# A graph attention layer on one core: weighted rows in a tile of their own, a carry that reads the sum ahead of its copy, and nine products without readers

## The chip, the core and the metric

The kernel runs on one core of a Trainium2 chip. A core has five engines with queues of their own: TensorE (PE in the profile, with PEld for its weight loads), VectorE (DVE), ScalarE (ACT), GpSimd (POOL) and SyncE (SP). They work in the order of their own queues and wait for each other by semaphores. The metric is the device time of one execution in microseconds; less is better.

## What is computed

One layer of graph attention over 12,500 nodes with 128 features and 200,000 edges that are sorted by destination.

```python
h = jnp.maximum(_layernorm(x), 0.0)
h = (h @ W_node.T).reshape(num_nodes, H, HD)              # H, HD = 4, 32
e = (edge_features @ W_edge.T).reshape(num_edges, H, HD)
att = jnp.sum(jnp.concatenate([h[src], h[tgt], e], -1) * a, axis=-1)
att = jnp.where(att > 0, att, 0.2 * att)
m = jnp.maximum(segment_max(att, tgt), 0.0)
ex = jnp.exp(att - m[tgt])
denom = segment_sum(ex, tgt) + (num_edges - deg)[:, None] * jnp.exp(-m)
h_prime = segment_sum((ex / denom[tgt])[:, :, None] * h[src], tgt)
out = x + h_prime.reshape(num_nodes, H * HD)
```

The sums divide by the denominator of the destination, so the kernel sums `ex * h[src]` and `ex` by destination and divides at the end.

## The kernel before, in words

**Tiling.** The sorted edges are cut into 392 groups of 511, each laid out as 512 places in four columns of 128 partitions (J = 4); the first place of a group holds what is carried in from the group before. A group's destinations fall into a window of at most 96 nodes (WIN). Four groups are a quad (98 quads), and two to four quads are a turned stage (`supers`: mostly four quads, 16 groups).

**First part.** Node features are normalised, multiplied by the weights and written to a table in DRAM, 137 numbers a row: the values with a one behind each head, a count, and the source's part of the logits (`R_SRC`). The first four quads gather raw rows of `x` meanwhile and convert them on the chip (`converted`).

**Gathers.** `gather` (L128) issues 16 indirect transfers per quad on POOL's queue (L137), one for each column of each group, into `ga`. This tile has room for eight quads (QUADS), that is 32 groups; the transfer into a group's slot must wait for the last use of that slot 32 groups earlier. `fetch(q + 2)` is called when the logits of quad q are opened.

**Logits.** `logits` (L493), for one group: DVE marks the destination of each edge (L500), TensorE picks the destination's part by these marks (L505) and adds the edge's part (L508). `add_sources` (L511), called by `flush` when the next quad's logits begin, reduces them and adds the source's part (L520, L522).

**Softmax, one turned stage at a time** (`softmax`, L533). The logits of up to 16 groups and four heads are turned so that edges lie along a row (L548); ACT makes 0.2 times the logits and DVE takes the larger (L550, L553); scans along the rows give the running maxima (L557, L582, L584), with two tiny products that move a column to a row and back (L564, L577); the exponentials are turned back (L600), as are the factors and the maxima of segment ends (L605, L610).

**Sums** (`sums`, L668), a step for each group: DVE weights the gathered rows in place, `ga` times `ex` (L687), and makes a one-hot matrix of the edges' windows places (L691). TensorE multiplies columns 1 to 3 of the group (L696, three products). Then `complete` (L621) finishes the group before it: DVE takes the last row of the sum before that one, scales it and writes it as the first row of `ga` (L634), ACT adds the count (L638), TensorE multiplies column 0 with it (L639), and ACT copies the finished sum from PSUM to SBUF (L640). This carry links each group to the next. After four groups `divide` (L701) makes the quotient on DVE and SP writes it out (L724).

**Order.** The order is written by hand: `together` runs the steps of several generators in turns. In a turned stage, the sums of one quad run beside the logits of a quad four or five ahead, and in the first quad of the stage also beside the softmax. So DVE's queue is, per group, L500, L687, L691, L634; PE's is L505 and L508, L696, L639; ACT's is L640 and L638. SP's queue holds, per quad, the loads of edges and destinations (L283, L285), four register loads (L458), eight window transfers (L468, L470), and four times a register load and a write of the result (L724).

Of the kernel before, what the change touches and what calls it, by code (L numbers as in the profile page):

```python
# [26 lines left out]
J = 4  # L27
# [19 lines left out]
def kernel(  # L47
# [68 lines left out]
    thru = consts.tile([1, G], F32, name="thru")  # L116
    flag = consts.tile([1, 1], I32, name="flag")
# [30 lines left out]
    with tc.manual_schedule():  # L148
# [88 lines left out]
        def converted(q, psum, turn_pool, copy):  # L237

            ga = GA[q]
            m = quads[q][1]  # L240
            made = []

            def turned_over(i):
                hT_ps = psum.tile([P, 512], F32, name="acc")
                hT_ps = hT_ps.rearrange("p (j e) -> p j e", j=J)
                for j in range(J):
                    nc.tensor.transpose(hT_ps[:, j, :], ga[:, i, j, 0:D], ident)
                hT = turn_pool.tile([P, J, P], F32, name="hT_e", bufs=2)
                copy(hT, hT_ps)
                made.append(hT)  # L250

            turned_over(0)
            for i in range(m):
                yield
                if i + 1 < m:
                    turned_over(i + 1)
                for k in range(J // 2):
                    row_ps = psum.tile([P, 512], F32, name="acc")
                    row_ps = row_ps.rearrange("p (j e) -> p j e", j=2)
                    for j in range(2):  # L260
                        nc.tensor.matmul(row_ps[:, j, :ROW], made[i][:, 2 * k + j, :],
                                         wcat, start=True, stop=True)
                    nc.scalar.copy(ga[:, i, 2 * k:2 * k + 2, :], row_ps[:, :, :ROW])
            rows = ga[:, :m].rearrange("p g j r -> p (g j) r")
            nc.scalar.copy(
                rows[:, :, 0:H * HW].rearrange("p t (h w) -> p t h w", w=HW)[:, :, :, HD],
                ones[:, 0:1].unsqueeze(2).to_broadcast([P, m * J, H]))
            nc.scalar.copy(rows[:, :, R_CNT], ones[:, 0:m * J])
            yield
# [18 lines left out]
        with tc.tile_pool(name="node", bufs=2) as node, tc.tile_pool(  # L288
# [10 lines left out]
            def indexed():  # L299
# [27 lines left out]
                yield  # L327

# [109 lines left out]
    with tc.tile_pool(name="work", bufs=2) as work, \  # L438
# [7 lines left out]
        share_ps = const_ps[0:WIN, WIN + G:].rearrange("p (g h) -> p g h", h=H)  # L446
        nc.vector.tensor_copy(lane_ps, lane)
        nc.vector.tensor_copy(node_ps, node_at)
        tops = consts.tile([1, H, len(supers) + 1], F32, name="tops")
# [7 lines left out]
        def window(g):  # L457
            return nc.values_load(  # L458
                base[0:1, g:g + 1], engines=[mybir.EngineType.SP], min_val=0, max_val=N - 1,
                skip_runtime_bounds_check_because="a destination, which is a node")  # L460

        def fetch_windows(q):
            g0, m = quads[q]
            pw = PW[q] = load.tile([WIN, QG, SIDE], BF16, name="pw")
            xw = XW[q] = work.tile([WIN, QG, D], F32, name="xw", bufs=8)
            at = [window(g0 + i) for i in range(m)]
            for i in range(m):
                nc.sync.dma_start(pw[:, i, :], side[bass.ds(at[i], WIN), :])  # L468
            for i in range(m):
                nc.sync.dma_start(xw[:, i, :], x[bass.ds(at[i], WIN), :])  # L470
# [14 lines left out]
        def open_logits(q):  # L485
            if q == supers[of_quad[q]][0]:
                fetch_rows(of_quad[q])
            if q + 2 < nq:
                fetch(q + 2)
            AT[q] = work.tile([WIN, QG, GE], BF16, name="at")  # L490
            LG[q] = ps.tile([P, QG, J, PIECES, H], F32, name="lg")
# [40 lines left out]

        def softmax(s):  # L533
# [11 lines left out]
            u = U.pop(s)  # L545
            t_ps = ps.tile([SBG * H, GE], F32, name="t_ps")
# [3 lines left out]
            nc.scalar.mul(low[:R], t_ps[:R, 1:GE], SLOPE)  # L550
            yield
            att = t_ps[:R, 1:GE]
            nc.vector.tensor_tensor(att, att, low[:R], op=OP.max)  # L553
# [23 lines left out]
            nc.tensor.matmul(col_ps, into[:, :R], ones[0:1, 0:1], start=True, stop=True)  # L577
            yield
# [7 lines left out]
            ex = turned.tile([SBG * H, GE], F32, name="ex")  # L586
# [20 lines left out]
            nc.scalar.copy(facs[:, :R], fac_ps)  # L607
# [3 lines left out]
            xs = turned.tile([P, J, SBG * H], F32, name="xs", bufs=2)  # L611
            nc.scalar.copy(xs[:, :, 0:R], top_ps)
# [5 lines left out]
        begun = []  # L618
        state = {}

        def complete():  # L621

            division = state.pop("division", None)
            if begun:
                complete_group(*begun.pop())
            if division:
                divide(*division)

        def complete_group(q, i, ga, hot, pt, acc, fc):
            g0, m = quads[q]  # L630
            g = g0 + i
            if g:
                before = state["before"]
                nc.vector.tensor_tensor(  # L634
                    ga[0:1, i, 0, 0:H * HW].rearrange("p (h w) -> p h w", w=HW),
                    before[WIN:WIN + 1, 0:H * HW].rearrange("p (h w) -> p h w", w=HW),
                    fc.unsqueeze(2).to_broadcast([1, H, HW]), op=OP.mult)
                nc.scalar.copy(ga[0:1, i, 0, R_CNT:R_CNT + 1], before[WIN:WIN + 1, R_CNT:R_CNT + 1])  # L638
            nc.tensor.matmul(acc, hot[:, i, 0, :], ga[:, i, 0, :], start=False, stop=True)  # L639
            nc.scalar.copy(pt[:, i, :], acc)  # L640
            state["before"] = acc

            part = 1 if q == nq - 1 else 2 if q == nq - 2 else QG
            if (i + 1) % part == 0 or i == m - 1:
# [4 lines left out]
                state["division"] = q, pt, den, lo, i + 1  # L649
# [6 lines left out]
        def marks(q):  # L656

            g0, m = quads[q]
            hot = work.tile([P, QG, J, WIN + 1], F32, name="hot", bufs=3)
# [8 lines left out]
        def sums(q):  # L668
# [10 lines left out]
            for i in range(m):  # L679
                nc.scalar.copy(ga[:, i, :, R_SRC:R_SRC + H], heads(xs)[:, :, :, g0 - s0 + i])  # L680
            for i in range(m):
                g = g0 + i
                if q == nq - 1 - FREE and i == 1:
                    for k in range(FREE):
                        HOT[nq - FREE + k] = marks(nq - FREE + k)
                val = ga[:, i, :, 0:H * HW].rearrange("p j (h w) -> p j h w", w=HW)
                nc.vector.tensor_tensor(  # L687
                    val, val, heads(ex)[:, :, :, g - s0].unsqueeze(3).to_broadcast([P, J, H, HW]),
# [6 lines left out]
                for j in range(1, J):  # L695
                    nc.tensor.matmul(acc, hot[:, i, j, :], ga[:, i, j, :], start=j == 1, stop=False)  # L696
                complete()
                begun.append((q, i, ga, hot, pt, acc, fc[:, :, g - s0]))
                yield

        def divide(q, pt, den, lo, hi):  # L701
# [20 lines left out]
            add.tensor_tensor(res[:, :n, :], res[:, :n, :], xw, op=OP.add)  # L722
            for i in range(n):
                nc.sync.dma_start(out[bass.ds(window(quads[q][0] + lo + i), WIN), :], res[:, i, :])  # L724

        def all_logits(q):
            flush()
            open_logits(q)
            for i in range(QG):
# [16 lines left out]
        def checked():  # L746
# [17 lines left out]
            for k, (g0, n) in enumerate(blocks(G, P)):  # L764
                rows = turned.tile([P, NE + 1], I32, name="rows")
                nc.scalar.dma_start(rows[:n], dst_rows[g0:g0 + n, 0:NE + 1])
                yield
# [16 lines left out]
        with tc.manual_schedule():  # L784
# [8 lines left out]
            for s, (q0, m) in enumerate(supers):  # L793
# [17 lines left out]
                if not s:  # L811
                    complete()
                    together(*late(3))
            flush()
            together(sums(nq - 1))
            complete()
            complete()
# [199 lines left out]
```

## Time and profile before

| what | value |
|---|---|
| three runs | 2570.87, 2578.58, 2586.93 us |
| profiled execution | 2600.19 us |
| its span, first to last instruction | 2598.4 us |
| busy: PE, PEld, DVE, ACT, POOL | 1405.4, 1256.7, 1367.0, 421.7, 1508.0 us |
| mean granted clock of TensorE | 0.536 |
| POOL's gathers from the table (L137) | 1502, 944 ns each (median), 161.1 to 2472.0 us |
| DMA | 299.12 MB, mean 115 GB/s |

Lines of the profile name an engine, a line of the kernel, the operation, and what is written and read (`acc<-ga,hot`), with the number of instructions and the time. In a list of waits a line says which engine idled before which instruction, whose signal ended that, and then the total in us, the number of waits and the longest. "remote" stands where the profile does not name the one that gave the signal, "issue" where it shows no wait. The end of a product of TensorE is modelled in these records; when its signal came is seen at the instruction that waits for it.

### The profile page before, as it was taken

To read this page: it belongs to the slowest core of one execution; us is meant where nothing else is said; L and a number is where in the kernel's file an instruction comes from. 1 tells how busy PE (TensorE), PEld (TensorE's weight loads), DVE (VectorE), ACT (ScalarE), POOL (GpSimd) and SP (SyncE) were. 2 spreads that over 40 slices of the span, in tenths; PEclk is the share of its full clock that TensorE was granted. 3 is DMA by queue.
4 is the path that set the end of the run, shared out by engine and by line. 5 is a ranking of instruction groups with operands and counts; after the bars stand their busy time and mean duration, and the time that the engine had idled before them with its cause. 6 is when DMAs were issued, how large, how long until landed. Compare 5 with 4: busy or idle time off the path is not lost. (4 is left out here: it accounts for less than half of the span.)

```text
span 2598.4 us, 29393 instructions
## 1 busy us (share of the span) xinstructions
PE 1405.4 (54%) x7275; PEld 1256.7 (48%) x7275; DVE 1367.0 (53%) x3291; ACT 421.7 (16%) x1806; POOL 1508.0 (58%) x1609
## 2 busy tenths in 40 slices
PE   2442665555555555556555555655555555545485
PEld 1331655545545445445445544545544554444375
DVE  2441465555555545555554554654554554555486
ACT  1431411111111111111111111111111111111122
POOL 7235256666666666666666666666666666666603
PEclk9975655555555555555555555555555555555555
DMA  4342455544544454554455445454544544434430
GB/s 150 102 126 53 108 136 124 127 116 118 128 123 113 115 142 107 127 125 117 119 124 124 116 119 123 120 125 117 125 115 118 125 121 116 121 97 112 103 92 17
DMA packets 214495, 299.12 MB, mean 115 GB/s; under 512 B 86121, under 2 KB 162153, under 8 KB 204914
## 3 DMA queue, kind: packets, MB, share of 16 engines
q1 hardware_dynamic: 162512, 184.97, 26.6%
q0 software_dynamic: 50112, 109.65, 19.3%
q10 hardware_dynamic: 1698, 2.58, 0.3%
q8 instruction: 61, 1.00, 0.2%
q14 instruction: 112, 0.92, 0.1%
HBM read 270.49 MB, written 26.52 MB: 114 GB/s over the span
## 5 line engine op out<-in xcount | busy, mean ns | idle before, releaser
L137 POOL DMA_INDIRECT ga<-table,srci x1502 | 1426.7, 950 | 963.2 <-issue 406.0
L696 PE MATMUL acc<-ga,hot 128*97 128x137 f32 x2352 | 649.6, 448 | 341.3 <-ACT ga L680 225.1
L696 PEld LDWEIGHTS acc<-ga,hot 128*97 128x97 f32 x2352 | 518.2, 279 | 366.1 <-ACT ga L680 229.2
L634 DVE TENSOR_TENSOR ga<-acc,facs 1x132 f32<-1x132 f32 x391 | 115.9, 296 | 625.9 <-ACT pt L640 502.1
L639 PE MATMUL acc<-ga,hot 128*97 128x137 f32 x784 | 267.4, 444 | 289.0 <-ACT ga L638 215.5
L508 PE MATMUL lg<-wblk,ea 128*128 128x8 f32 x1568 | 410.5, 360 | 0.0
L508 PEld LDWEIGHTS lg<-wblk,ea 128*128 128x128 f32 x1568 | 383.3, 310 | 0.0
L505 PEld LDWEIGHTS <-at 96*128 96x128 bf16 x1568 | 219.7, 167 | 298.7 <-DVE at L500 115.0
L639 PEld LDWEIGHTS acc<-ga,hot 128*97 128x97 f32 x784 | 190.3, 279 | 320.3 <-ACT ga L638 235.8
L640 ACT COPY pt<-acc 97x137 f32<-97x137 f32 x392 | 107.4, 274 | 1431.8 <-remote 850.5
L505 PE MATMUL lg<-pw,at 96*128 96x12 bf16 x1568 | 170.7, 182 | 239.1 <-DVE at L500 101.2
L687 DVE TENSOR_TENSOR ga<-ga,ex_ps 128x528 f32<-128x528 f32 x392 | 270.0, 689 | 8.4 <-remote 8.0
L500 DVE TENSOR_TENSOR at<-const_ps,db 96x512 bf16<-96x512 f32 x392 | 267.1, 683 | 9.0 <-DMA db<-in_dst_dram 3.2
L691 DVE TENSOR_TENSOR hot<-const_ps,slot 128x384 f32<-128x384 f32 x384 | 209.4, 545 | 0.0
L520 DVE TENSOR_REDUCE st<-lg 128x64 f32<-128x192 f32 x98 | 35.0, 358 | 139.1 <-remote 109.7
L638 ACT COPY ga<-acc 1x1 f32<-1x1 f32 x391 | 59.9, 153 | 228.8 <-DVE ga L634 114.1
L375 PE MATMUL row_ps<-wcat,hT 128*128 128x137 f32 x198 | 40.3, 354 | 79.9 <-DVE hT L367 32.0
L600 PE MATMUL ex_ps<-ident,ex 64*128 64x64 f32 (+2 forms) x112 | 18.6, 315 | 115.6 <-ACT ex L589 49.7
L375 PEld LDWEIGHTS row_ps<-wcat,hT 128*128 128x128 f32 x198 | 34.0, 246 | 86.1 <-issue 46.0
L553 DVE TENSOR_TENSOR t_ps<-t_ps,low 64x511 f32<-64x511 f32 (+2 forms) x28 | 19.2, 687 | 104.4 <-issue 60.2
L137 POOL DMA_INDIRECT ga<-in_x_dram,srci x64 | 60.6, 947 | 20.9 <-issue 19.2
L600 PEld LDWEIGHTS ex_ps<-ident,ex 64*128 64x128 f32 (+2 forms) x112 | 13.8, 208 | 118.3 <-ACT ex L589 51.1
(131 smaller groups left out, 1131.1 us busy)
## 6 DMA issues: line engine op xcount, KB each, us to landing
db<-in_dst_dram SPq DMA_DIRECT2D x98, 768.0 KB
ea<-in_edge_t_dram SPq DMA_DIRECT2D x98, 512.0 KB
ga<-table,srci POOLq DMA_INDIRECT x1502
xw<-in_x_dram SPq DMA_DIRECT2D x392, 48.0 KB
out_dram<-res SPq DMA_DIRECT2D x392, 48.0 KB
pw<-side SPq DMA_DIRECT2D x392, 2.2 KB
table<-row SPq DMA_DIRECT2D x9, 616.5 KB
xt<-in_x_dram SPq DMA_DIRECT2D x9, 576.0 KB
```

Source lines behind the costliest of these rows:

```text
L137: nc.gpsimd.indirect_dma_start(out=ga[:, i, j, 0:width], out_offset=None, in_=rows, in_offset=bass.IndirectOffsetOnAxis(ap=srci[:, g0 + i, ...
L375: nc.tensor.matmul(row_ps[:, t, :ROW], hT[:, t, :], wcat, start=True, stop=True)
L500: nc.vector.tensor_tensor(at[:, i, :], node_ps[0:WIN, g0 + i:g0 + i + 1].to_broadcast([WIN, GE]), db[:, i, :], op=OP.is_equal)
L505: nc.tensor.matmul(lg[:, i, j].rearrange("p k h -> p (k h)"), at[:, i, j * P:(j + 1) * P], sw, start=i + j == 0, stop=False, skip_group_ch ...
L508: nc.tensor.matmul(lg[:, i, 2 * w:2 * w + 2, 0, :], ea[:, i, w, :], wblk, start=False, stop=True, skip_group_check=True)
L634: nc.vector.tensor_tensor(ga[0:1, i, 0, 0:H * HW].rearrange("p (h w) -> p h w", w=HW), before[WIN:WIN + 1, 0:H * HW].rearrange("p (h w) -> ...
L638: nc.scalar.copy(ga[0:1, i, 0, R_CNT:R_CNT + 1], before[WIN:WIN + 1, R_CNT:R_CNT + 1])
L639: nc.tensor.matmul(acc, hot[:, i, 0, :], ga[:, i, 0, :], start=False, stop=True)
L640: nc.scalar.copy(pt[:, i, :], acc)
L687: nc.vector.tensor_tensor(val, val, heads(ex)[:, :, :, g - s0].unsqueeze(3).to_broadcast([P, J, H, HW]), op=OP.mult)
L691: nc.vector.tensor_tensor(hot[:, i, :, 0:WIN], lane_ps.unsqueeze(1).to_broadcast([P, J, WIN]), slot[:, g, :].unsqueeze(2).to_broadcast([P, ...
L696: nc.tensor.matmul(acc, hot[:, i, j, :], ga[:, i, j, :], start=j == 1, stop=False)
```

## The change

1. **Weighted rows in a tile of their own.** DVE's weighting reads `ga` and writes `gw2`, which holds two groups and has two buffers. The products, the carried row and the appended columns (count and maxima) use `gw`. The count of a gathered row isn't read any more.
2. **The carry.** `complete_group` lets DVE take the carried row from the sum ahead of ACT's copy of it. The copy (`copied`) comes a step later, and a division another step later (`divisions`, which count down), except in the last two quads. The carried count is made once for all groups by a scan (`came`), and comes into `gw` with the maxima (`xs_all`), one copy for two groups.
3. **Softmax.** The slope is applied by one DVE operation before the turn; ACT's L550 and DVE's L553 fall away. `facs` is copied by DVE, one row of it.
4. **Logits.** `lg` is one tile with two halves for even and odd quads; the first group's marks and products come before `flush`.
5. **Register loads of SP** for the windows are read by one call per quad or division.
6. **Last quads.** Their one-hot matrices are made on POOL a quad at a time, one quad ahead.
7. **Products without readers.** `run_on` multiplies the identity by ones into the unused half of `lg`: eight products after the last stage's column product (L577 before), and one after its last turn.

The lines of the changed kernel stand higher: the weighting is L727, the one-hot matrix L732, the products of columns 1 to 3 L737, the carried row L667, the product of column 0 L671, the copy L676.

```diff
@@ indexed
+                own_ps = wide_ps[0][0:1, :]
+                for j in range(J):
+                    nc.tensor.matmul(own_ps, ones_b, is_last[:, :, j], start=j == 0, stop=j == J - 1)
+                nc.vector.memset(came[:, 0:1], 0.0)
+                yield
+                nc.vector.tensor_tensor_scan(came[:, 1:G + 1], thru, own_ps, initial=0.0,
+                                             op0=OP.mult, op1=OP.add)
@@ fetch_windows
-            at = [window(g0 + i) for i in range(m)]
+            at = windows(q)
@@ open_logits
-            LG[q] = ps.tile([P, QG, J, PIECES, H], F32, name="lg")
+            LG[q] = lg_all[:, q % 2]
@@ run_on
+            unread = lg_all[:, nq % 2].rearrange("p i j k h -> p (i j k h)")[:, 0:P]
+            for _ in range(n):
+                nc.tensor.matmul(unread, ident, ones, start=True, stop=True)
@@ softmax
+            nc.vector.scalar_tensor_tensor(u[:, :, :R], u[:, :, :R], SLOPE, u[:, :, :R],
+                                           op0=OP.mult, op1=OP.max)
...
-            nc.scalar.mul(low[:R], t_ps[:R, 1:GE], SLOPE)
             yield
             att = t_ps[:R, 1:GE]
-            nc.vector.tensor_tensor(att, att, low[:R], op=OP.max)
...
             nc.tensor.matmul(col_ps, into[:, :R], ones[0:1, 0:1], start=True, stop=True)
+            if s == len(supers) - 1:
+                run_on(8)
...
-            nc.scalar.copy(facs[:, :R], fac_ps)
+            nc.vector.tensor_copy(facs[WIN:WIN + 1, :R], fac_ps[WIN:WIN + 1, :])
...
+            if s == len(supers) - 1:
+                run_on(1)
+            xs = xs_all[:, s % 2]
+            nc.scalar.copy(xs[:, :, 1:, 0:m], top_ps.rearrange("p j (h g) -> p j h g", h=H))
+            nc.scalar.copy(xs[0:1, 0, 0, 0:m], came[:, g0:g0 + m])
@@ complete
-            division = state.pop("division", None)
+            due = [d for d in divisions if d[0] >= nq - 2 or d[-1] == 1]
+            divisions[:] = [d[:-1] + (1,) for d in divisions if d not in due]
+            full = state.pop("full", None)
             if begun:
                 complete_group(*begun.pop())
-            if division:
-                divide(*division)
+            if full:
+                copied(*full)
+            for d in due:
+                divide(*d[:-1])
@@ complete_group
-                    ga[0:1, i, 0, 0:H * HW].rearrange("p (h w) -> p h w", w=HW),
+                    gw[0:1, 0, 0:H * HW].rearrange("p (h w) -> p h w", w=HW),
...
-                nc.scalar.copy(ga[0:1, i, 0, R_CNT:R_CNT + 1], before[WIN:WIN + 1, R_CNT:R_CNT + 1])
-            nc.tensor.matmul(acc, hot[:, i, 0, :], ga[:, i, 0, :], start=False, stop=True)
+            nc.tensor.matmul(acc, hot[:, i, 0, :], gw[:, 0, :], start=False, stop=True)
+            state["before"] = acc
+            state["full"] = q, i, pt, acc
+
+        def copied(q, i, pt, acc):
             nc.scalar.copy(pt[:, i, :], acc)
...
-                state["division"] = q, pt, den, lo, i + 1
+                divisions.append((q, pt, den, lo, i + 1, 2))
@@ sums
-            for i in range(m):
-                nc.scalar.copy(ga[:, i, :, R_SRC:R_SRC + H], heads(xs)[:, :, :, g0 - s0 + i])
...
-                if q == nq - 1 - FREE and i == 1:
-                    for k in range(FREE):
-                        HOT[nq - FREE + k] = marks(nq - FREE + k)
-                val = ga[:, i, :, 0:H * HW].rearrange("p j (h w) -> p j h w", w=HW)
+                if i == 1 and nq > q + 1 >= nq - FREE:
+                    HOT[q + 1] = marks(q + 1)
+
+                if i % 2 == 0:
+                    gw2 = work.tile([P, 2, J, ROW], F32, name="gw")
+                    n = min(2, m - i)
+                    nc.scalar.copy(
+                        gw2[:, 0:n, :, R_CNT:R_SRC + H],
+                        xs[:, :, :, g - s0:g - s0 + n].rearrange("p j h g -> p g j h"))
+                gw = gw2[:, i % 2]
+                by_head = lambda t: t[:, :, 0:H * HW].rearrange("p j (h w) -> p j h w", w=HW)
                 nc.vector.tensor_tensor(
-                    val, val, heads(ex)[:, :, :, g - s0].unsqueeze(3).to_broadcast([P, J, H, HW]),
+                    by_head(gw), by_head(ga[:, i]),
+                    heads(ex)[:, :, :, g - s0].unsqueeze(3).to_broadcast([P, J, H, HW]),
                     op=OP.mult)
...
-                    nc.tensor.matmul(acc, hot[:, i, j, :], ga[:, i, j, :], start=j == 1, stop=False)
+                    nc.tensor.matmul(acc, hot[:, i, j, :], gw[:, j, :], start=j == 1, stop=False)
@@ divide
+            at = windows(q, lo, hi)
             for i in range(n):
-                nc.sync.dma_start(out[bass.ds(window(quads[q][0] + lo + i), WIN), :], res[:, i, :])
+                nc.sync.dma_start(out[bass.ds(at[i], WIN), :], res[:, i, :])
@@ all_logits
+            open_logits(q)
+            logits(q, 0)
+            yield
             flush()
-            open_logits(q)
-            for i in range(QG):
+            for i in range(1, QG):
```

## The prediction

> **What bounds the kernel now.** I read the page's busy rows first, then the stretches of one turned stage, then the waits, then the timeline of one stretch of gathers.
>
> ```profile
> core 0: us, PE busy (x) PEld busy (x) DVE busy (x) ACT busy (x) POOL busy (x), PEclk, DMA share, GB/s
> 1207.00:1303.00 96.00, 53.82 (x278) 48.69 (x278) 51.66 (x118) 12.82 (x63) 61.01 (x66) 0.50 0.50 121
> 1303.00:1399.00 96.00, 53.14 (x275) 47.55 (x273) 50.79 (x115) 12.51 (x62) 60.54 (x64) 0.50 0.49 118
> 2475.00:2508.50 33.50, 27.46 (x148) 25.20 (x148) 29.34 (x69) 7.51 (x34) 0.00 (x0) 0.50 0.42 109
> ```
>
> One turned stage of four quads (16 groups, 64 gathers) takes 96.0 us, 6.0 a group, and no engine is over 64% busy in it. The last line is two quads after POOL's last gather (2472.9): 33.5 us for 8 groups, 4.2 a group, with PE and DVE 82% and 88% busy. The same work runs 30% faster once POOL is silent. So what POOL does is part of the bound.
>
> ```profile
> ACT pt L640 <- remote: 850.5, 102, 11.9
> POOL ga L137 <- issue: 425.2, 1394, 0.6
> POOL ga L137 <- remote: 245.4, 100, 3.3
> POOL ga L137 <- PE acc L639: 146.5, 46, 15.2
> ```
>
> The waits say who: ACT's copy of a finished sum waits 850 us in 102 waits, and POOL waits 245 and 146 us. The timeline shows what they wait for:
>
> ```profile
> 1300.34 0.94 POOL L137 DMA_INDIRECT ga<-table,srci  x1 [2.16 <-remote]
> ...
> 1304.04 0.66 PE L639 MATMUL acc<-ga,hot 128*97 128x137 f32 x2
> ...
> 1304.74 0.27 ACT L640 COPY pt<-acc 97x137 f32<-97x137 f32 x1 [1.72 <-PE acc L639]
> ...
> 1306.96 0.66 PE L639 MATMUL acc<-ga,hot 128*97 128x137 f32 x2
> ...
> 1314.06 0.94 POOL L137 DMA_INDIRECT ga<-table,srci  x1 [0.30 <-issue]
> ...
> 1317.61 0.27 ACT L640 COPY pt<-acc 97x137 f32<-97x137 f32 x1 [11.85 <-remote]
> 1317.84 0.95 POOL L137 DMA_INDIRECT ga<-table,srci  x1 [2.84 <-remote]
> ```
>
> POOL starts a run of gathers at 1300.34. The product of 1304.04 is told to ACT within 0.04 us. The product of 1306.96 ends in the record at 1307.62, yet ACT learns of it at 1317.61, ten us later, and only after POOL had issued its twelfth gather and stood still from 1315.00. I sorted all such pairs between 420 and 2470 us by the age of the run. Up to 4 us after a run's start TensorE's signals are 0.04 us late; from 5 us on nearly all are late by 2 to 10 us, and most of these come when POOL has stopped, some 2.1 to 2.6 us after its last gather. The same is seen in the first 240 us, where POOL gathers without a stop and copies wait 10 to 23 us for products that are over.
>
> So there is a cycle. POOL issues one gather per 0.94 + 0.30 = 1.245 us, as long as slots of its ring of 32 groups are free. A slot is freed by the last product (L639) of the group 32 earlier. Signals get stuck, POOL runs out of slots, stops, the signals flood, POOL goes on. A stage is 64 x 1.245 = 79.7 us of issuing plus 16.3 us in seven waits of 2.3 us (runs of 12, 12, 8, 8, 4, 12, 8 gathers). The time is POOL's issuing, which the change does not touch, plus these waits.
>
> **The change part by part.**
>
> *Weighted rows in a tile of their own (gw), so that a slot of ga is freed by DVE's product (L687's successor) instead of TensorE's L639.* In DVE's order the weighting of group g+2 stands ahead of the carry of g+1 (L634), which waits for L639 of g. So when L639 of g is stuck, POOL can fill up to the slot of g+2, where before it stopped ahead of the slot of g: a ring longer by three groups, worth nothing in a steady cycle. But the wait at the end of a run gets longer. Before, the L639 that POOL needs is in the flood itself, and POOL starts 0.23 us after ACT. After, when the flood comes, DVE must first do L634 (0.30), the marks of L500 (0.69) and the weighting (0.69), then POOL is released: 1.68 + 0.24 = 1.9 us later. Once in four groups a division (0.17 + 0.17 + 0.18 + 0.26 + 0.68 + 0.69 with gaps, 2.4 us) stands between: 0.6 on average. A wait becomes about 2.2 + 1.9 + 0.6 = 4.7 us in place of 2.3.
>
> How many waits? They pay by giving TensorE prompt signals. Before: the flood, then products ending 1.4 and 4.4 us into the run, and the next at 7.3 is stuck: three groups per wait at best, 16/7 = 2.3 in fact. After: flood, then by the same durations (L639 0.46, lg 1.05, L696 1.4 on PE, 2.9 a group; 2.25 on DVE) products ending 1.1, 4.4 and 7.3 us after the flood, which is -0.8, 2.5 and 5.4 us into the run. The third misses the 4 to 5 us by little. In its favour: of the three products of L696 only the last one now raises a signal that is waited for (2248 signals of TensorE in the program before, 1397 after), so that signals which trickle through one by one carry the chain further. I take four groups per wait (three if none trickles through, five if two do): 4 x 4.7 = 18.8 us against 16.3, +2.5 us a stage, and over 2050/96 = 21.4 stages +54 us. With three groups: 5.3 x 4.7 = 25 us, +186. With five: 3.2 x 4.7 = 15 us, -27.
>
> Here a rule speaks differently. The Trainium skill, "SBUF — State Buffer", section "Who interferes with whom", says that only the port pair shared by VectorE and GpSimd causes contention, and that TensorE shares its ports with no one. By it the late signals have nothing to do with POOL, the chain of carries is slow by itself, and each hop removed pays: ACT's L640 (0.27) and L638 (0.15) and two hand-overs, 0.6 us x 343 groups = -206 us. The rows speak against it: the same chain at 4.2 us a group after POOL's end with the hops in it. I take the rows and keep the rule as a rival.
>
> *The carry reads the sum before ACT copies it; the count comes from a scan (came) made once; the copy and the division come one and two steps later.* They take L640 and L638 out of the chain (391 x 0.15 us of ACT fall away). Under the cycle above these are hidden behind POOL's run; in the last 125 us PE and DVE are the limit. ACT is 13% busy in a stage, so what moves to or from it (six rows fewer per quad, the copies of the scales and maxima in pairs) costs nothing; if DVE waited for it, the copies in front of the pair's weighting (0.27 + 0.22 + 0.3) still lie beside L520, L522 and L500 (1.3 us).
>
> *The slope on u (128x256, one DVE operation) for ACT's L550 and DVE's L553.* New operation: nearest row L594, 32x511 at 0.68 us, half the elements, 0.4 us. It removes 0.59 + 0.69 and a hand-over: about -1.3 us in each of 28 stages, hidden in all but the last five or six: -7 us.
>
> *lg in two halves, the first marks before the flush.* DVE's L520 stood up to 9.3 us for a stuck product; it then stands a group later. What is late next is the carry behind the same stuck signals, so nothing is counted; the cover is POOL's run.
>
> *Windows read together.* 785 register loads of SP become 201. They sit ahead of transfers whose readers come two quads later (only 2.7 us of waits for pw in the trace): nothing. Were SP late, PE's L505 would show it.
>
> *came, in the node stage:* four bf16 products, one scan of 392 elements (L557: 511 elements, 1.21 us), memsets: 0 to +2 us, take +1.
>
> *Marks of the last quads one quad at a time, no wait of their own:* POOL has its gathers behind it there (64 us idle), nothing.
>
> *Nine products without readers.* Nearest row: six of L696 in 1.69 us, 0.28 each; eight products are sixteen instructions of 0.23 (start to start): 3.6 us, into a stretch where PE stood 4.23 us for ex (2561.45 to 2565.68). Cost 0 to +1. What they may give is the clock:
>
> ```profile
> 2554.39 1.69 PE L696 MATMUL acc<-ga,hot 128*97 128x137 f32 x6 [2.52 <-DVE hot L691]
> ...
> 2557.29 0.95 PE L696 MATMUL acc<-ga,hot 128*97 128x137 f32 x6
> ```
>
> The second fell into 3.4 us of full clock: 0.74 us saved by six instructions. The last seven groups could save 7 x 1 us if it held. The skill's "TensorE: Matmul & The Clock Gate" (Part 1, the HAM clock gate) has the full clock come after about 3.4 us of sustained work in a window that runs freely, and go after an idle one; by that 3.6 us of products are just one window, caught or missed. Between -7 and +1 I take -2, nearest to the trace, where such stretches last 3.4 us.
>
> *The tail.* POOL ends three groups further ahead; they run at 4.2 instead of 6.0 us: -5.
>
> Sum: +54 - 7 + 1 - 2 - 5 = +41 us. The profiled execution took 2600.2 us (span 2598.4 and 1.8 around it), 0.8% above the median 2578.6. 2641 x 0.9917 = 2619, rounded to 2620 us.
>
> **The rivals.**
>
> *Faster: the waits shrink.* DVE frees slots early enough that POOL's stops stay at 2.3 us and only four are needed: 9.2 us a stage, -7.1 x 21.4 = -152, with the small items (-13) 2600 - 165 = 2435, 2415 as a median. Or the chain is the bound after all: -206, about 2365. The floor with no waits is -349 us, 2230. For it: 1397 signals in place of 2248, the shorter chain. Against it: POOL's release now needs work of DVE that begins after the flood.
>
> *Clearly slower, the far side of the same mechanism:* no signal trickles through, three groups or fewer per wait: +186 - 13, 2773, 2750 as a median; with as many waits as now, 7 x 4.7 = 33 us, +357, 2920. It decides from 3.5 groups per wait downward.
>
> *No change:* five groups per wait, -27 - 13: 2560, 2539 as a median; with four and a half it comes to about 2578. That the change doesn't do what it says is no rival: in the changed program's order POOL's gathers wait for DVE's weighting.
>
> **How the numbers follow.** Forecast (four groups per wait, 2570 to 2680) 0.45; slower beyond it 0.25; faster 0.30. The range leaves out the faster half of the fast case and the far end of the slow one: 2440 to 2790. Within 1% (2553 to 2604, about what three runs spread over 0.6% can tell) lie the lower part of the forecast and the upper of the fast case: 0.20. Faster 0.28, slower 0.52.
>
> **What would show it.** Right: POOL's gathers wait for DVE's weighting, with waits near 4 to 5 us, three to five a stage; runs of 12 to 20 gathers; a stage of 97 to 101 us; no long wait of ACT's copy, and in its place DVE's carry waiting for L639's successor up to 10 us. Wrong: waits of POOL still near 2.3 us and fewer, a stage under 93 us; or TensorE's signals prompt while POOL gathers, which would take away the ground of all this.

## The result and the profile after

The changed kernel took 2829.86 us (median of 4, 2823.14 to 2833.62) beside 2575.08 us (median of 4, 2570.87 to 2586.93) for the kernel before: a ratio of 1.098, 95% interval 1.093 to 1.102. It is slower, as forecast, but by 255 us instead of 41, and outside the range.

The stretches of the kernel after, as shown of before: two whole turned stages, and 33.5 us behind POOL's last gather.

```profile
core 0: us, PE busy (x) PEld busy (x) DVE busy (x) ACT busy (x) POOL busy (x), PEclk, DMA share, GB/s
1207.00:1313.00 106.00, 54.36 (x274) 47.47 (x274) 50.97 (x116) 8.73 (x37) 60.67 (x65) 0.50 0.44 109
1313.00:1419.00 106.00, 54.35 (x274) 47.45 (x274) 51.03 (x116) 8.73 (x37) 60.50 (x65) 0.50 0.43 109
2679.00:2712.50 33.50, 26.57 (x138) 24.01 (x138) 27.50 (x67) 5.17 (x21) 0.00 (x0) 0.50 0.30 81
```

A stage now takes 106 us instead of 96, with the same products, gathers and clock. Behind POOL's last gather the work runs at nearly the old pace (67 operations of DVE in 33.5 us beside 69), so most of the loss is not there. The waits of the kernel after:

```profile
ACT pt L676 <- DVE gw L667: 1438.4, 249, 17.1
DVE gw L667 <- remote: 830.7, 109, 14.8
...
POOL ga L140 <- DVE gw L727: 574.0, 96, 10.9
...
POOL ga L140 <- issue: 439.1, 1414, 2.1
```

What stood as a wait of ACT's copy for 850 us is now DVE's carry L667 waiting for 831 us: the same late signals, met one engine earlier. ACT's 1438 us are idle time in front of a copy that only a later division reads. POOL's two waits of before (245 and 147 us) have become one, for DVE's weighting, of 574 us. The spans differ by 222.9 us: POOL's last gather ends at 2675.9 instead of 2472.9 us (+203), and what follows it takes 145 us instead of 126 (+20).

I took POOL's pauses from the trace (every gap between two gathers over the usual 0.3 us, behind 420 us, without that 0.3). Before: 148 pauses of 2.27 us in the mean, 336 us. After: 97 of 5.58 us, 541 us. The difference, 205 us, is the +203. One pause of each kind, in the timeline of the kernel after:

```profile
1206.80 0.94 POOL L140 DMA_INDIRECT ga<-table,srci  x1 [0.30 <-issue]
1210.79 0.30 DVE L667 TENSOR_TENSOR gw<-acc,facs 1x132 f32<-1x132 f32 x1 [10.33 <-remote]
1211.12 0.69 DVE L519 TENSOR_TENSOR at<-const_ps,db 96x512 bf16<-96x512 f32 x1
...
1211.73 0.69 DVE L727 TENSOR_TENSOR gw<-ga,ex_ps 128x528 f32<-128x528 f32 x1
...
1212.69 0.94 POOL L140 DMA_INDIRECT ga<-table,srci  x1 [4.95 <-DVE gw L727]
...
1253.30 0.95 POOL L140 DMA_INDIRECT ga<-table,srci  x1 [0.30 <-issue]
1256.60 0.15 DVE L607 COPY col<-ex_ps 64x1 f32<-64x1 f32 x1 [6.64 <-remote]
1256.85 1.28 DVE L609 TENSOR_TENSOR_SCAN t_ps<-kp,col,t_ps 64x511 f32<-64x511 f32 x1
1258.16 1.22 DVE L611 TENSOR_TENSOR_SCAN t_ps<-kp,t_ps 64x511 f32<-64x511 f32 x1
...
1259.41 0.68 DVE L615 TENSOR_TENSOR ex<-low,t_ps 64x511 f32<-64x511 f32 x1
...
1262.56 0.23 DVE L634 COPY facs<-acc 1x64 f32<-1x64 f32 x1 [0.78 <-PE acc L632]
1262.82 0.70 DVE L727 TENSOR_TENSOR gw<-ga,ex_ps 128x528 f32<-128x528 f32 x1
...
1263.79 0.94 POOL L140 DMA_INDIRECT ga<-table,srci  x1 [9.55 <-DVE gw L727]
```

The first pause is the one that the prediction worked out: POOL stops at 1207.74, the flood comes 3.05 us later, then carry, marks and weighting 1.9 us. The second is another: the flood brings the product behind the column step of the softmax (L602 to L607), and DVE does the two scans, the subtraction, waits for ACT and for TensorE, and only then the weighting: 7.2 us between flood and gather. Of the 97 pauses 20 hold this column step (all that are over 8 us; 9.4 us in the mean, 187 us together), 19 hold the softmax's first step with the slope (6.5 us, 124 us), the other 58 have 4.0 us in the mean and 4.5 in the median.

### The profile page after: what moved, and what is told of

It is laid out like the page before. It is cut to its first block, busy times and chain, and to the rows that moved or that the text cites. A ratio compares the mean times of both kernels' runs of the same rounds, so it can differ in the third digit from the quotient of the medians.

```text
span 2821.3 us, 27008 instructions
## 1 busy us (share of the span) xinstructions
PE 1423.4 (50%) x7297; PEld 1242.7 (44%) x7297; DVE 1369.7 (49%) x3323; ACT 323.6 (11%) x1187; POOL 1502.3 (53%) x1609
## 3 DMA queue, kind: packets, MB, share of 16 engines
q0 software_dynamic: 50112, 109.65, 16.2%
## 4 chain that ended last, share of the span: by engine, by line
another core or an unknown queue 34%; DVE 29%; PE 17%; issue 8%; POOL 3%; ACT 1%; DMA 1%; SPq 1%; DVEq 0%; POOLq 0%
PE acc L737 7%; DVE at L519 5%; DVE gw L727 5%; PE lg L527 4%; DVE hot L732 4%; PE acc L671 3%; DVE gw L667 3%; POOL ga L140 3%; DVE res L763 2%; DVE res L759 2%; DVE t_ps L609 1%; DVE t_ps L611 1%; DVE run L621 1%; PE lg L524 1%
## 5 line engine op out<-in xcount | busy, mean ns | idle before, releaser
L737 PE MATMUL acc<-gw,hot 128*97 128x137 f32 x2352 | 643.9, 445 | 65.6 <-issue 15.6
L671 PE MATMUL acc<-gw,hot 128*97 128x137 f32 x784 | 268.5, 445 | 670.3 <-DVE gw L667 557.7
L667 DVE TENSOR_TENSOR gw<-acc,facs 1x132 f32<-1x132 f32 x391 | 115.9, 296 | 938.7 <-remote 830.7
L737 PEld LDWEIGHTS acc<-gw,hot 128*97 128x97 f32 x2352 | 515.3, 278 | 96.9 <-issue 53.5
L671 PEld LDWEIGHTS acc<-gw,hot 128*97 128x97 f32 x784 | 185.1, 274 | 712.8 <-DVE gw L667 587.0
L524 PEld LDWEIGHTS <-at 96*128 96x128 bf16 x1568 | 211.8, 164 | 303.3 <-DVE at L519 139.0
L676 ACT COPY pt<-acc 97x137 f32<-97x137 f32 x392 | 107.1, 273 | 1883.3 <-DVE gw L667 1438.4
L727 DVE TENSOR_TENSOR gw<-ga,ex_ps 128x528 f32<-128x528 f32 x392 | 270.7, 690 | 1.3
L732 DVE TENSOR_TENSOR hot<-const_ps,slot 128x384 f32<-128x384 f32 x384 | 210.0, 547 | 0.0
L699 POOL TENSOR_SCALAR hot<-lane,slot 128x96 f32<-128x96 f32 x32 | 17.0, 552 | 105.3 <-ACT hot L695 94.2
L759 DVE TENSOR_TENSOR res<-pt,const_ps 96x512 f32<-96x512 f32 (+2 forms) x102 | 67.5, 662 | 5.9 <-DMA out_dram<-res 1.6
```

The source lines that it names most:

```text
L524: nc.tensor.matmul(lg[:, i, j].rearrange("p k h -> p (k h)"), at[:, i, j * P:(j + 1) * P], sw, start=i + j == 0, stop=False, skip_group_ch ...
L667: nc.vector.tensor_tensor(gw[0:1, 0, 0:H * HW].rearrange("p (h w) -> p h w", w=HW), before[WIN:WIN + 1, 0:H * HW].rearrange("p (h w) -> p ...
L671: nc.tensor.matmul(acc, hot[:, i, 0, :], gw[:, 0, :], start=False, stop=True)
L727: nc.vector.tensor_tensor(by_head(gw), by_head(ga[:, i]), heads(ex)[:, :, :, g - s0].unsqueeze(3).to_broadcast([P, J, H, HW]), op=OP.mult)
L732: nc.vector.tensor_tensor(hot[:, i, :, 0:WIN], lane_ps.unsqueeze(1).to_broadcast([P, J, WIN]), slot[:, g, :].unsqueeze(2).to_broadcast([P, ...
L737: nc.tensor.matmul(acc, hot[:, i, j, :], gw[:, j, :], start=j == 1, stop=False)
```

## The experiments

Each kernel ran beside the kernel before on one chip, in one session. The kernel before itself took 2575 us in the result above, 2027 to 2034 us (medians) in some sessions of the experiments, and 2577 to 2609 (medians) in the others. Nothing lies between, and within a session it stayed at the one or the other. One and the same chip showed both a few minutes apart, so it isn't the chip. I call these prompt and late sessions, by TensorE's signals; the recorded expectations say "call" for a session. In the traces of prompt sessions no signal of TensorE that ended a wait came more than 0.02 us behind the end of its product in the records; in late ones they came up to 10.2 us behind it (before) and 11.8 us (after). Which of the two a kernel would meet couldn't be chosen. None of the experiments' kernels met two late sessions, so how far a session by itself moves a late ratio isn't known.

**e1, e2, e3, e4 (a prompt session).** e1 puts the weighted rows back into ga, e2 gives the kernel before a gw alone, e3 and e4 leave the gathers out.

```
# e1, on the kernel after
-                    gw2 = work.tile([P, 2, J, ROW], F32, name="gw")
+                    gw2 = ga[:, i:i + 2]
# e2, on the kernel before (and gw for ga in L634, L638, L639, L696; marks one quad at a time;
# hot with two buffers instead of three)
+                if i % 2 == 0:
+                    gw2 = work.tile([P, 2, J, ROW], F32, name="gw")
+                    n = min(2, m - i)
+                    for k in range(n):
+                        nc.scalar.copy(gw2[:, k, :, R_SRC:R_SRC + H],
+                                       heads(xs)[:, :, :, g - s0 + k])
+                    nc.scalar.copy(gw2[:, 0:n, :, R_CNT], ones[:, 0:n * J])
+                gw = gw2[:, i % 2]
...
-                    val, val, heads(ex)[:, :, :, g - s0].unsqueeze(3).to_broadcast([P, J, H, HW]),
+                    by_head(gw), by_head(ga[:, i]), heads(ex)[:, :, :, g - s0].unsqueeze(3).to_broadcast([P, J, H, HW]),
# e3 and e4, in gather(), on the kernels before and after
+        if q >= QUADS:
+            return
```

> The changed kernel with its rows weighted in place in ga again, no gw; everything else of the change stays. Theory (POOL's slots are freed by DVE's weighting, which stands behind the flood, the next marks, the division and the softmax step; that alone costs): POOL waits for TensorE's L671 again, a wait shrinks from 5.5 to about 2.3 us. If the waits stay at four a stage, a stage is 79.7 + 9.2 = 89 us and the time (106 - 89) x 21.4 = 360 us under the changed kernel's: about 2460; if they go back to seven, 96 us a stage and about 2600. Rival (the later copy and division, or the carry ahead of the copy, cost the time): still 2780 to 2840.

> The kernel before with weighted rows in a tile gw of their own, filled by the weighting, ACT's copies of the scales and one copy of ones, and the marks of the last quads made one quad at a time (two buffers of hot, to make room); the carry, copy and division stay as before. Theory (freeing a slot by DVE's weighting costs): POOL waits for L727's counterpart, waits of 5 us and more, 2750 to 2900 us. Rival (it is the rest of the change that costs): 2550 to 2600.

> The kernel before without the gathers after the first 32 groups (1440 of 1566 left out, the ring's old rows are used again), and with the weighting as an addition instead of a product, which takes as long. Theory (gathering holds TensorE's signals back): signals are prompt throughout, no copy waits 10 us, a group takes 4.2 to 4.4 us as behind POOL's last gather, in place of 6.0: about 2575 - 1.7 x 350 = 1980 us. Rival (the chain of carries is slow by itself, whatever POOL does): no faster than 2500 us.

> The changed kernel without the gathers after the first 32 groups, nothing else changed. Theory: signals are prompt, the changed kernel is then no slower than the kernel before in the same state: 1900 to 1980 us, 4.2 us a group. Rival (gw or the order of DVE's work is slow in itself, without POOL): over 2500 us, or at least 100 us above the kernel before without gathers.

Measured: the kernel before 2029.27 us, e1 2034.5 (ratio 1.0029, 1.0018 to 1.0040), e2 2037.25 (1.0044, 1.0027 to 1.0061), e3 1653 and e4 1687 us (one run each). Neither theory had a number for e1 and e2 in a prompt session. Without gathers both kernels are faster, and faster than expected (1980; 1900 to 1980), but the changed one by less, 34 us above the other: there is no gain in its chain that gathers merely hide. e4's stretch (columns as above):

```profile
907.00:1003.00 96.00, 81.49 (x429) 74.98 (x430) 80.77 (x183) 13.98 (x60) 0.00 (x0) 0.50 0.48 113
```

PE and DVE are 85% and 84% busy, much as behind POOL's last gather in the kernel before (82% and 88%).

**e5: the changed kernel itself (a prompt session).**

> The changed kernel itself once more, beside the kernel before. In the runs of e1 and e2 the kernel before took 2029 us, not 2575, and no signal of TensorE was late while POOL gathered. Theory (the change costs only where signals are late, by what POOL's waits grow): where the kernel before takes about 2030, POOL never waits and the changed kernel takes 2025 to 2045; where the kernel before takes about 2575, 2830 again. Rival (the change costs 250 us wherever it runs): 2250 to 2300 beside 2030.

Measured: 2033.72 us beside 2029.78 (1.0022, 1.0012 to 1.0032). The theory holds for this kind of session, the rival falls: the change costs 4 us here. From its waits:

```profile
POOL ga L140 <- issue: 408.0, 1338, 0.5
...
DVE gw L667 <- PE acc L671: 46.3, 139, 1.9
```

From 420 us to POOL's last gather no gap between two gathers is over 0.32 us. The carry L667, which waited 831 us for late signals in the result, waits 46 us here, 1.9 at most. No signal is late, POOL's issuing alone sets the end (1566 gathers at 1.245 us are 1950 of the 2030 us), and who frees a slot doesn't matter.

**e7 and e8 (a late session).** e7 writes the next group's weighting behind complete(), inside a quad; e8 drops the two uses of run_on.

```
# e7
                 complete()
                 begun.append((q, i, gw, hot, pt, acc, fc[:, :, g - s0]))
+                if i + 1 < m:
+                    soon = weigh(i + 1)     # the former lines of gw2, the copy and the weighting
                 yield
```

> The changed kernel with the next group's weighting placed in DVE's order directly behind the carry of the group before, ahead of the next marks and of whatever softmax or division step stands there (within a quad; the first group of a quad as before). Theory (POOL's waits are long for the work of DVE between the flood and the weighting): where the kernel before takes about 2575, the waits that are 5 to 9 us lose L519 (0.6) and the first half of the softmax step (2.4), some 4.5 us a stage of 106, about 100 us: 2700 to 2760 against 2830. Where the kernel before takes about 2030, POOL never waits: 2025 to 2045. Rival (the length of POOL's waits is set by the late signals alone): 2820 to 2840 in the first case.

> The changed kernel without the nine products that nobody reads. The prediction's step (they give 2 us at most 7, through a faster clock in the last groups): 2 us slower than the changed kernel, which stood 4 us over the kernel before where that takes 2030: so 6 us over it, or up to 11. Rival (they cost what they take, or nothing): 3 to 4 us over the kernel before.

Measured: before 2608.75, e7 2950.78 (one run), e8 2979.73 us (1.1438, 1.1416 to 1.1460). e7 misses both its numbers; those of e8 were meant for a prompt session. In e8 67 of 89 pauses of POOL hold the division, as this one:

```profile
1256.49 0.95 POOL L140 DMA_INDIRECT ga<-table,srci  x1 [0.30 <-issue]
1260.70 0.30 DVE L663 TENSOR_TENSOR gw<-acc,facs 1x132 f32<-1x132 f32 x1 [10.11 <-remote]
1261.02 0.17 DVE L745 TENSOR_SCALAR others<-pt 96x4 f32<-96x4 f32 x1
...
1262.73 0.69 DVE L759 TENSOR_TENSOR res<-res,xw 96x512 f32<-96x512 f32 x1
1263.34 0.68 DVE L519 TENSOR_TENSOR at<-const_ps,db 96x512 bf16<-96x512 f32 x1
1263.94 0.69 DVE L723 TENSOR_TENSOR gw<-ga,ex_ps 128x528 f32<-128x528 f32 x1
...
1264.90 0.95 POOL L140 DMA_INDIRECT ga<-table,srci  x1 [7.46 <-DVE gw L723]
```

POOL does 16 gathers (in front of 76 of the 89 pauses), one quad, and stops at the same place of each quad, and there the division stands between carry and weighting: 4.2 us from flood to gather instead of 1.9. 21 pauses hold the column step, 16 of them together with the division (11.9 us in the mean). With four groups to a pause the pauses lock to a place in the quad, and meet the same work of DVE each time or never: in the trace of the kernel after, 7 of 97 pauses hold a division. That the nine products have to do with the place is not shown, since no late session had both e8 and the kernel after. Against it stands e7, which has the products and in the same session met the division in 63 of its 107 pauses. What the nine products do where they stand can be read: from POOL's last gather to the end e8 takes 145.6 us, the kernel after 145.4. Against the division e7 could not help: it stands in the last step of a quad, and the weighting behind it is the next quad's first, which e7 leaves in its place. Where a moved weighting stands directly behind the carry (22 pauses), a pause is 3.1 us.

**e9, e10, e11 (a prompt session).** e9 puts the weighting directly behind the carry, ahead of the copy and the division, also into the next quad of a stage.

```
             if begun:
                 complete_group(*begun.pop())
+            then()
             if full:
                 copied(*full)
...
-                complete()
+                complete(lambda: weigh_next(q, i))
```

> The changed kernel with the next group's weighting directly behind the carry, ahead of the copy's division too, and over quads of one stage. In the two kernels before this one POOL stood 7.5 us in most waits, each with the same DVE work between the flood and the weighting: carry, division, marks, weighting, 4.2 us. Theory (that work is what the waits are too long by): 4.2 becomes 1.3, a wait 4.4, four a stage 18 to 20 us with the one at the softmax step: a stage of 98 to 100 us, 2640 to 2700. Rival (POOL's waits only lock to another place in the quad, or their length comes from the signals): 2830 and more. Where the kernel before takes 2030: 2025 to 2045.

> The changed kernel with its rows weighted in place in ga again (as e1), for a call in which TensorE's signals are late while POOL gathers, which shows in the kernel before: about 2600 us, not 2030. Theory (POOL's wait ends with DVE's weighting, behind whatever DVE has to do between the flood and it; in place it ends with L671, which is in the flood itself): waits of 2 to 2.5 us; with four a stage about 2460, with seven about 2600, in either case at least 200 under the changed kernel. Rival (the change costs by its carry, copy and division): as the changed kernel, 2830 to 2980. Where the kernel before takes 2030: 2034 again.

> The changed kernel itself, beside the two above. Where the kernel before takes about 2600: 2830 if it locks as in its first trace (waits of 4.5, 4.8, 6.8 and 9.2 us a stage), 2960 to 2990 if it locks as without the nine products (waits of 7.5 us on the division): then the nine products, which stand in the last stage alone, have nothing to do with the 150 us between the two. Rival (the nine products save them): 2830 only. Where the kernel before takes 2030: 2034.

Measured: before 2032.87, e9 2033.09 (1.0003, 0.9996 to 1.0011), e10 2037.66 (1.0021, 1.0010 to 1.0031), the kernel after 2037.64 (1.0025, 1.0011 to 1.0039). That told nothing of late signals, so e10 ran again as e12 (prompt, 1.0028) and e13, and e9 as e14 and e15 (prompt, 1.0004 and 1.0008) and e16.

**e13: in place (a late session).**

> In place, the same kernel, for a call in which the kernel before takes about 2600. New since e7 and e8: POOL's signals-to-come take 1.8 us after a run of 8 gathers, 2.5 after 12, 3.0 to 3.1 after 16, so the first part of a wait depends on the run. Theory: in place a wait is that part alone; runs of 12 to 16 give four to five waits of 2.5 to 3 us, 11 to 14 us a stage, 2480 to 2540; runs as before (seven waits of 2.3), 2600. Rival (carry, copy and division cost the time): 2830 to 2980. Where the kernel before takes 2030: 2034 again.

Measured: 2647.1 us beside 2577.88 (1.026, 1.022 to 1.031). It lies between the two expectations (at most 2600, at least 2830): the pauses are short again, but not few enough.

```profile
1313.28 0.94 POOL L140 DMA_INDIRECT ga<-table,srci  x1 [0.30 <-issue]
1316.63 0.30 DVE L667 TENSOR_TENSOR ga<-acc,facs 1x132 f32<-1x132 f32 x1 [5.61 <-remote]
...
1317.34 0.94 POOL L140 DMA_INDIRECT ga<-table,srci  x1 [3.11 <-ACT pt L676]
```

From flood to gather it is 0.7 us in the median, not 1.9 to 7.2. So gw accounts for most of the loss, and the rest of the change, the late copy and division among it, for about 2.6%.

**e16: the weighting directly behind the carry (a late session).**

> The same kernel as e9, e14 and e15 (next weighting directly behind the carry), for a call in which the kernel before takes about 2600. Theory: a wait of POOL is 3.0 + 1.0 us but for the softmax step's, a stage 97 to 100 us: 2620 to 2720. Rival (the waits lock so that other work stands in between, or gw holds POOL in another way): 2800 to 2980. Where the kernel before takes 2030: 2033 again.

Measured: 2850.45 us beside 2594.25 (1.099, 1.096 to 1.102). The theory's number is missed by over 130 us, and the time is the changed kernel's. Yet the edit did what it should:

```profile
1320.73 0.29 DVE L668 TENSOR_TENSOR gw<-acc,facs 1x132 f32<-1x132 f32 x1 [3.13 <-PE acc L759]
1321.05 0.70 DVE L724 TENSOR_TENSOR gw<-ga,ex_ps 128x528 f32<-128x528 f32 x1
...
1322.03 0.94 POOL L140 DMA_INDIRECT ga<-table,srci  x1 [3.78 <-DVE gw L724]
```

From flood to gather it is 1.3 us in the median. But there are 122 pauses in place of 97, and 21 are still over 8 us (224 us together): at the column step the weighting needs that step's own result and can't be moved ahead of it, and in 10 of the 21 a division stands in front as well (12.9 us in the mean). The waits show a new one as well:

```profile
DVE gw L668 <- remote: 621.6, 88, 14.0
ACT gw L720 <- remote: 597.7, 57, 15.0
...
POOL ga L140 <- DVE gw L724: 456.3, 79, 14.3
```

L720 is ACT's copy of the scales into the next pair of gw, now placed where it waits for a late signal itself. So this run doesn't show a gain for less work of DVE in the pause. What it shows is that the pauses without column step and division became shorter (3.3 us against 4.5) and more (101 against 72). A reading that fits is that POOL's pause is also the time in which TensorE gets its signals through: cut short, it lets fewer groups pass. That is argued, not shown.

**e17: gw alone on the kernel before (e2 in a late session).**

> The kernel before with gw alone (as e2), for a call in which the kernel before takes about 2600. Known by now: the whole change 1.098, without gw (in place) 1.026, with the weighting first 1.099. Theory (gw makes POOL wait for DVE's weighting, behind the late signal and DVE's other work; the carry's place matters little): 1.06 to 1.11, 2730 to 2870, waits of POOL of 4 us and more. Rival (gw costs only together with the later copy and division): 0.98 to 1.03, 2530 to 2660. Where the kernel before takes 2030: 2037 again.

Measured: 2718.93 us beside 2576.61 (1.056, 1.053 to 1.059), 11 us below the theory's interval; the rival falls. The edit also gives `hot` two buffers instead of three, as the change itself does and e13 with it, so this is not told apart from the rest in either. The waits:

```profile
ACT pt L640 <- remote: 1278.3, 142, 15.3
...
POOL ga L137 <- DVE gw L692: 460.5, 112, 8.2
```

The late sessions together, with POOL's pauses counted as above and scaled to the 64 gathers of a stage:

| kernel | time beside before | pauses in 64 gathers | mean, us | together, us | all pauses over 8 us |
|---|---|---|---|---|---|
| before | 1 | 6.9 | 2.27 | 15.7 | 0 |
| the change without gw (e13) | 1.026 | 5.6 | 3.16 | 17.7 | 1 |
| gw alone (e17) | 1.056 | 5.9 | 3.56 | 20.9 | 0 |
| the change | 1.098 | 4.5 | 5.58 | 25.3 | 20 |
| the change, weighting first (e16) | 1.099 | 5.7 | 4.55 | 25.9 | 21 |
| the change, next weighting earlier inside a quad (e7, one run) | 1.131 | 5.0 | 6.23 | 31.1 | 5 |
| the change without nine products (e8) | 1.144 | 4.2 | 7.50 | 31.1 | 24 |

The time goes with the fifth column: the changed kernel's 9.6 us more in a stage, over 21.4 stages, are 205 of the 223 us between the two traces. gw alone costs 5.6%, the rest 2.6%, both 9.8%. No pause of e13 or e17 holds the column step (the copy L607 and the scans behind it); with both parts 20 or 21 do, one in a stage, and in all but e7 nearly all pauses over 8 us are these. Why it takes both is not settled.

**e18 and e19: the kernel after without gathers, for a late session.**

> The changed kernel without the gathers after the first 32 groups (as e4, which took 1687 where the kernel before took 2029), for a call in which the kernel before takes about 2600. Theory (signals of TensorE are late there only while POOL gathers): signals prompt, 1680 to 1700 as in e4, plus what the first 128 gathers cost, at most 60 us. Rival (TensorE's signals are late there for another reason, and POOL only waits for them): 2500 us and more. Where the kernel before takes 2030: 1687 again.

Both met prompt sessions and took 1686 and 1687 us, as e4. Whether a late session has late signals without gathers stays open; what speaks against it is only that in the late traces no signal is over 0.1 us late behind POOL's last gather. What makes a session late stays open too. None of these kernels is faster than the kernel before in either kind of session.

## Why the prediction was right in direction and wrong in size

*What held.* POOL waits for DVE's weighting; the late signals are met by the carry and no more by ACT; runs of 16 gathers are the commonest (12 to 20 were named). Pauses in a stage: four forecast, 4.5 measured, and the plain ones, 58 of 97, have a median of 4.5 us where 4.7 was worked out. That closeness is in part luck: their first part was longer than forecast, most held no division, and the pauses are counted here without POOL's usual 0.3 us.

*The step that failed* is the length of a wait: "about 2.2 + 1.9 + 0.6 = 4.7 us". It was 5.6 in the mean. The 1.9 is there to the tenth. The 2.2 is 2.9 (median), since it grows with the run in front of it and the runs got longer. The 0.6 took only the division as what can stand between flood and weighting, spread evenly; the division was met in 7 pauses of 97, and the softmax step, which the sum doesn't have at all, in 39: 19 of 6.5 us and 20 of 9.4. In us: 97 x 5.58 = 541, against 21.4 x 18.8 = 402 in the sum. Of the 139 between them some 85 come from the length and 53 from the count (4.53 waits in a stage instead of four). These 139, the 13 us by which the pauses of before were put too high (349 against 336), and 25 us of the tail are 177 of the 182 us by which the trace's +223 passes the sum's +41.

*The tail* was put at -5 and came to +20: behind POOL's last gather gw leaves 33 carries (144 us in e17, 145 after), in place 31 are left (131 us), as before (126). What follows the last carry takes 14.9 us instead of 10.6, in place too (15.0); the cause of that is open.

*The small terms.* The nine products, -2: nothing (0.2 us between the two tails; the eight ran from 2780.3 to 2784.1 us, the granted clock stayed at 0.50 from 2779.6 to 2793.1, and from 2790 to 2800 it was 0.67, beside 0.69 in the same stretch without them, e8). The slope on u, -7: not seen; it became part of the 6.5 us pauses, with 0.42 us in each. The scan for came with all else of the change costs 4 to 5 us where POOL never waits (e5, e11).

*The rivals.* "Clearly slower" was put at 2750 and tied to 3.5 groups per wait; with 16 / 4.53 = 3.5 groups it came to lie at that point, but more by longer waits than by their number (85 and 53 us of the 139). "Faster" fell in both its forms. The rule of the Trainium skill ("SBUF — State Buffer", "Who interferes with whom"), kept as a rival, agrees with the prompt sessions, where TensorE isn't disturbed by POOL, but its -206 us don't come there, since POOL's issuing is then the bound, nor without gathers (e4 is 34 us above e3). The late sessions' signals, up to 11.8 us late, are not explained by a rule of ports; there the rows were right against the -206.

*What the prediction took for the kernel's own* was its ground, signals that are late while POOL gathers. It named prompt signals as a sign of being wrong, but not that it could be the session that decides: the same program has late signals or not, and the change costs 9.8% or 0.2%.

## What to carry to other kernels

When the release of a buffer is moved from one engine to another, list everything that stands in the new engine's order between the event that ends the wait and the releasing instruction, stage by stage, the rare steps too; a periodic wait locks to one place in the order, so that such work counts each time or never, not by its average. The length and the number of waits are not independent: here shorter pauses only became more of them. And before a mechanism is taken as the kernel's, see it in a second session: here the same program ran in 2030 or in 2600 us.

## What the runs showed of the hardware

The same gathers in the same program leave TensorE's signals prompt in some sessions and hold them back in others. A gather takes 0.94 to 0.95 us in both. The packets of the gathers' queue took 457 and 501 us of each DMA engine in late sessions (after: 16.2% of 2821 us; before: 19.3% of 2598) and 501 and 511 us in prompt ones (e1: 24.7% of 2030; e5: 25.2% of 2029). So it is not the transfers that get slower.

Only TensorE's signals are late. I compared each signal that ended a wait of over 0.15 us, between 420 us and the last gather, with the end of the instruction that gave it. Of TensorE's, 281 of 545 came more than 0.5 us behind (before) and 159 of 267 (after); of the signals of DVE and ACT, in the same stretches, none of 747 and none of 1000 came more than 0.03 us behind.

In late sessions the first late signal comes the later after POOL's stop, the longer POOL had run: 1.84 us after 8 gathers (62 cases, before), 2.52 after 12 (65, before), 2.99 after 16 (44, after; 3.00 in e17) and 3.66 after 20 (9, after), medians: some 0.15 us more for each gather. Runs of four, which follow another pause closely, don't fit: 1.52 us (21 cases, before) and 2.49 (12, after). A prompt session shows nothing of it: in e5 no signal of TensorE is over 0.02 us late, with over a thousand gathers on end.
